# One set of expert lists for four chunks: 39 blocks in three classes in place of 46 in two groups

## The chip, the core and the metric

The kernel runs on one core of a Trainium2 chip. The time is device time of one execution in microseconds (us); the time of a kernel is the median of several executions. A separate execution under the hardware profiler gives the trace. The engines are PE (TensorE, matrix products and transposes, with its weight loads as PEld), DVE (VectorE), ACT (ScalarE), POOL (GpSimd) and SP (SyncE, which here only issues transfers). ACT and POOL issue transfers too: ACT writes results of blocks, POOL does the transfers whose rows are picked by an index. 16 DMA engines carry out all of them.

## What is computed

`x` has 32 x 64 = 2048 tokens of 512 values. Two layers follow each other, each an attention to `ctx_4096` and a feed-forward part. The part that matters here is the last one, a mixture of eight experts, each a 512 x 512 matrix, of which a token uses the best two:

```python
def _L1_ffn_ref(x, W_gate, b_gate, W_e, b_e):
    TOP_K = 2
    logits = x @ W_gate + b_gate
    _, top_idx = jax.lax.top_k(logits, TOP_K)
    y_all = jax.nn.relu(jnp.einsum('bsd,edh->bseh', x, W_e) + b_e)
    y = jnp.take_along_axis(y_all, top_idx[..., None], axis=2)
    return y.mean(axis=2)

x = x + _L0_xattn_ref(_layernorm(x), ctx_4096, ...)
x = x + _L0_ffn_ref(_layernorm(x), ...)
x = x + _L1_xattn_ref(_layernorm(x), ctx_4096, ...)
x = x + _L1_ffn_ref(_layernorm(x), L1_ffn_W_gate, L1_ffn_b_gate, L1_ffn_W_e, L1_ffn_b_e)
```

All data are float32.

## The kernel before

The tokens are handled in four chunks (`NC`) of 512, each of four tiles (`TT`) of 128 tokens. `xs[i]` is tile i of the residual stream, which stays in SBUF. The first attention, the first feed-forward part and the second attention take the kernel up to about 1800 us. The second attention runs as 32 attention blocks, eight for each chunk; the routing of chunk c goes on during the attention blocks of chunk c + 1.

**Routing of a chunk** (`route_step`). Its steps are "rows" (layer norm), "turn" (transpose), "logits", "ranks" (which two experts each token keeps, `keep`) and "places". `route_places` counts, for each expert, how many tokens came before: products with a triangle of ones and with all ones (`cnt`), then running sums (`run`, `counts`, `pos`). `chosen` makes two row numbers for each token from these (`at`): the start of the expert's list in DRAM plus the token's place in it. `route_row` then scatters 128 normed rows into the lists `xg` by these numbers; four tiles and two experts for each token make eight scatters a chunk. They are put on the list `sends` and sent a few at a time.

**Lists and blocks.** The experts' lists are cut into blocks of 128 rows, so that one product of a block uses one expert's matrix. The number of blocks that the loop runs is fixed when the kernel is built, while the counts are only known on the chip; the number is therefore an upper bound, and the last blocks may be empty. There are two groups (`GROUPS`): chunks 0 to 2, and chunk 3, each with its own lists `xg[i]` and results `yg[i]`. `NB` is 2 x 1536 / 128 + 7 = 31 blocks for the first and 2 x 512 / 128 + 7 = 15 for the second. `close_lists(i)` makes a table `bi` on DVE once the counts of a group are complete: for each block its expert and its first row in DRAM. For the first group it stands in the attention block 6 of the last chunk, for the second one in slot 13 of the block loop.

**The block loop.** Slot m loads rows (`load_rows`, every fourth slot for four blocks, on SP, from an address read out of the table), transposes block m (`block_turn`, PE, copied out of PSUM by ACT as `xT`) and multiplies block m - 1 with its expert (`block_expert`): four products on PE into a PSUM bank `py`, of which there are two, the bias added by DVE (`y`), Relu with the factor 0.5 on ACT, and a write to `yg` from ACT's queue. The routing steps of chunk 3 are spread over the first slots (`between`), with one scatter a slot from slot 9 on.

**The way back.** `token_rows` makes, for each token, the two rows of `yg` that hold its results. `gather` fetches them with two indexed transfers of 128 rows from POOL's queue, `combine` adds the two and adds them to the residual on DVE, and SP stores the tile to `out`. The twelve tiles of the first group are gathered one in each slot from slot 34 on and combined two slots later, in three buffers (`t4`); the four tiles of chunk 3 follow after the loop.

**Order.** Work on an engine runs in the order in which the scheduler puts it; what is wrapped in `pin` keeps the order of the program on its engine. Products, transposes, bias adds, sums and all the list arithmetic are pinned. A load by an address from the table waits for all scatters of its group (`add_manual_dep`), and a scatter for the clearing of the lists, which SP does with zeros during the first attention (`clear_lists`).

Of the kernel before, what the change touches and what calls it, by code (L numbers as in the profile page):

```python
# [16 lines left out]
P = 128  # L17
# [12 lines left out]
def layers(ctx: ExitStack, tc: tile.TileContext, a: dict, out: bass.AP):  # L30
# [235 lines left out]
    GROUPS = [range(0, NC - 1), range(NC - 1, NC)]  # L266
    CAP = [len(cs) * CH for cs in GROUPS]
    NB = [2 * cap // P + NE - 1 for cap in CAP]
    xg = [dram.tile([NE * cap, HID], F32, name=f"xg{i}") for i, cap in enumerate(CAP)]
    yg = [dram.tile([nb * P, HID], F32, name=f"yg{i}") for i, nb in enumerate(NB)]  # L270

    start_row = const.tile([P, 2, NE], F32, tag="start_row", name="start_row")
    for i, cap in enumerate(CAP):
        nc.gpsimd.iota(
            start_row[:, i, :], pattern=[[cap, NE]], base=0, channel_multiplier=0,
            allow_small_or_imprecise_dtypes=True,
        )
# [3 lines left out]
    clearings = ([], [])  # L281
    waits = mybir.DependencyInfo(mybir.DependencyClass.Sync, mybir.DependencyReason.DATA)

    def clear_lists(e):
        for i, cap in enumerate(CAP):
            ins = nc.sync.dma_start(
                xg[i][e * cap : (e + 1) * cap, :].rearrange("(p m) (k n) -> p (m k) n", p=P, n=P),
                zero[:, None, :].broadcast_to([P, cap // P * KT, P]),
            )
            clearings[i].append(ins.ins)  # L290
# [338 lines left out]
    for i in range(len(order) + 1):  # L629
# [33 lines left out]
        else:  # L663
# [10 lines left out]
            if i % 4 == 1:  # L674
                clear_lists(i // 4)
# [352 lines left out]
    counts, slots = {}, {}  # L1028
# [33 lines left out]
    def route_places(c, keep):  # L1062

        n = f"e{c}"
        i = 0 if c in GROUPS[0] else 1
# [8 lines left out]
        if i in counts:  # L1074
            pin(nc.vector.tensor_copy(run[:, 0, :], counts[i]))
        else:
            pin(nc.vector.memset(run[:, 0, :], 0.0))
        for t in range(TT):
            pin(nc.vector.tensor_tensor(run[:, t + 1, :], run[:, t, :], tot[:, 1, t, :], ALU.add))
        counts[i] = run[:, TT, :]  # L1080
# [3 lines left out]
        return chosen(pos, keep, start_row[:, i, :], n)  # L1084
# [3 lines left out]
    scatters = ([], [])  # L1088

    def route_row(c, h, at, t, r):  # L1090
        i = 0 if c in GROUPS[0] else 1
        ins = pin(
            nc.gpsimd.indirect_dma_start(
                out=xg[i],
                out_offset=bass.IndirectOffsetOnAxis(ap=at[:, r, t : t + 1], axis=0),
                in_=h[:, t, :],
                in_offset=None,
            )
        )
        for other in scatters[i]:  # L1100
            tc.declare_no_dep(ins.ins, other, reason="rows of a list are distinct")
        for clearing in clearings[i]:
            tc.add_manual_dep(ins.ins, clearing.name, waits, reason="cleared before")
        scatters[i].append(ins.ins)

    def chosen(pos, keep, offset, name):

        q = small.tile([P, TT, NE], F32, tag="q", name=f"q_{name}", bufs=2)
        pin(nc.vector.tensor_tensor(q, pos, offset[:, None, :].broadcast_to([P, TT, NE]), ALU.add))
# [9 lines left out]
    def close_lists(i):  # L1119

        n = f"l{i}"
        top = CAP[i] // P
        lst = small.tile([P, 3, NE], F32, tag="lst", name=f"lst_{n}", bufs=2)
        cmp = small.tile([P, NE, 12], F32, tag="cmp", name=f"cmp_{n}", bufs=1)
        pin(nc.vector.tensor_scalar(lst[:, 2, :], counts[i], 1.0 / P, None, ALU.mult))
        pin(
            nc.vector.tensor_tensor(
                cmp[:, :, 0:top],
                lst[:, 2, :, None].broadcast_to([P, NE, top]),
                steps[:, None, 0:top].broadcast_to([P, NE, top]),  # L1130
                ALU.is_gt,
            )
        )
        pin(nc.vector.tensor_reduce(lst[:, 0, :], cmp[:, :, 0:top], AX.X, ALU.add))
        pin(
            nc.vector.tensor_tensor(
                cmp[:, :, 0:NE], lst[:, 0, None, :].broadcast_to([P, NE, NE]), earlier, ALU.mult
            )
        )
        pin(nc.vector.tensor_reduce(lst[:, 1, :], cmp[:, :, 0:NE], AX.X, ALU.add))  # L1140
        pin(nc.vector.tensor_tensor(lst[:, 2, :], lst[:, 0, :], lst[:, 1, :], ALU.add))

        nb = NB[i]
        own = small.tile([1, 32, NE], F32, tag="own", name=f"own_{n}", bufs=1)[:, 0:nb, :]
        blk = small.tile([1, 4, 32], F32, tag="blk", name=f"blk_{n}", bufs=1)[:, :, 0:nb]
        pin(
            nc.vector.tensor_tensor(
                own,
                lst[0:1, 2, None, :].broadcast_to([1, nb, NE]),
                steps[0:1, 0:nb, None].broadcast_to([1, nb, NE]),  # L1150
                ALU.is_le,
            )
        )
        pin(nc.vector.tensor_reduce(blk[:, 0, :], own, AX.X, ALU.add))
        pin(nc.vector.tensor_scalar(blk[:, 0, :], blk[:, 0, :], float(NE - 1), None, ALU.min))
        pin(
            nc.vector.tensor_tensor(
                own, own, lst[0:1, 0, None, :].broadcast_to([1, nb, NE]), ALU.mult
            )
        )  # L1160
        pin(nc.vector.tensor_reduce(blk[:, 1, :], own, AX.X, ALU.add))
        pin(nc.vector.tensor_tensor(blk[:, 1, :], steps[0:1, 0:nb], blk[:, 1, :], ALU.subtract))
        pin(
            nc.vector.tensor_scalar(
                blk[:, 1, :], blk[:, 1, :], float(top - 1), float(P), ALU.min, ALU.mult
            )
        )
# [12 lines left out]
    def load_rows(i, j0, bi):  # L1180
        xr = t8(f"xr_{i}_{j0}")
        for j in range(j0, min(j0 + 4, NB[i])):
# [6 lines left out]
            for ins in scatters[i]:  # L1189
                tc.add_manual_dep(load.ins, ins.name, waits, reason="all rows are written")  # L1190
# [279 lines left out]
```

## Time and profile before

| | us |
|---|---|
| median of 3 runs | 2008.15 |
| runs | 2007.62 to 2009.62 |
| profiled execution | 2011.58 |
| its span, first to last instruction | 2009.9 |
| PE busy in the span | 1939.5 (96%) |
| 46 products of blocks (`py`), PE busy | 165.8 |
| first transposes of a block | at 1804.29 |
| last bias add of a block | at 1986.85 |
| 32 gathers, first and last issue | at 1933.62 and 2000.40 |

"Busy" is the time in which an engine carries out instructions. Idle time is put down to what ended it, the releaser. The chain of waits follows the work that ended last back through what released it, so that the time on it is time that the end depended on. A window gives the busy time of each engine in a stretch, the clock that TensorE was granted (1.00 is full speed), the mean busy share of the 16 DMA engines and what they moved. That share counts packets, and packets that overlap can take it over 1.

### The profile page before, as it was taken

What the parts mean: (1) busy time and instruction counts of PE and PEld (TensorE: products, weight loads), DVE (VectorE), ACT (ScalarE), POOL (GpSimd) and SP (SyncE); (2) the same over time, 40 slices, a digit from 0 to 9 for tenths busy, and PEclk for the clock granted to TensorE, in tenths of its full rate; (3) what the DMA queues carried; (4) which work ended last, traced back from release to release, by engine and by line L of the source; (5) the groups of instructions that cost most, each with busy time, mean ns of one, the idle gap of its engine ahead of it and who ended that gap; (6) DMA issues with size and microseconds to landing.
All of it is one profiled execution on the core that took longest, in us unless ns stands there. A gap on an engine that the chain in (4) does not pass through costs nothing.

```text
span 2009.9 us, 26460 instructions
## 1 busy us (share of the span) xinstructions
PE 1939.5 (96%) x10576; PEld 1539.5 (77%) x10576; DVE 1014.9 (50%) x1961; ACT 494.4 (25%) x935; POOL 475.0 (24%) x502
## 2 busy tenths in 40 slices
PE   6999999999999999999999999999999999879995
PEld 5888888888888888888888887777787767655442
DVE  7445345345356544444444445364456576762324
ACT  1211111111111221121121122221222655533221
POOL 5111111111122111111111120142145545541024
PEclk8999999999999999999999999999999999989998
DMA  9894110110210110110110013000004101325457
GB/s 320 249 291 131 53 37 16 53 35 19 73 55 21 53 32 22 53 32 22 53 32 22 22 58 105 1 0 11 1 22 157 43 17 53 111 85 183 152 167 231
DMA packets 138234, 155.39 MB, mean 77 GB/s; under 512 B 5121, under 2 KB 88897, under 8 KB 138113
## 3 DMA queue, kind: packets, MB, share of 16 engines
q1 hardware_dynamic: 126096, 124.53, 19.9%
q0 software_dynamic: 5392, 17.11, 2.7%
q10 hardware_dynamic: 6624, 12.06, 1.6%
q8 instruction: 85, 1.39, 0.3%
q14 instruction: 37, 0.30, 0.1%
HBM read 94.44 MB, written 58.20 MB: 76 GB/s over the span
## 4 chain that ended last, share of the span: by engine, by line
PE 90%; DVE 6%; ACT 2%; POOL 1%; issue 1%; DMA 1%; POOLq 0%; SPq 0%; DVEq 0%; ACTq 0%
PE ppx_o L425 11%; PE pqx_a L425 8%; PE py L105 8%; PE sc_a L105 6%; PE pqz_a L425 6%; PE pv_a L105 6%; PE ppz_o L425 5%; PE pk_a L105 5%; PE po_o L105 3%; PE ppy_o L425 3%; PE pdx_f L425 3%; PE pqv_a L425 3%; PE pqy_a L425 3%; PE pp L105 3%; PE phx_f L425 2%; PE pq_b L105 1%
## 5 line engine op out<-in xcount | busy, mean ns | idle before, releaser
L105 PE MATMUL py<-arena,xT 128*128 x368 | 165.8, 593 | 0.2 <-ACT xT L1200 0.2
L407 POOL TENSOR_TENSOR arena<-weights 128x512 f32<-128x512 f32 x16 | 20.3, 1269 | 563.2 <-PE ppz_o L425 563.2
L366 ACT ACTIVATE at_a<-at_a 128x512 f32<-128x512 f32 x64 | 40.4, 631 | 444.0 <-DVE at_a L365 444.0
L105 PEld LDWEIGHTS pv_a<-weights,arena 128*128 128x128 f32 x1024 | 119.4, 192 | 15.3 <-issue 15.3
L425 PE MATMUL pqz_a<-arena 128*128 128x256 f32 x512 | 122.8, 383 | 4.4 <-DVE qT_a L501 4.4
L105 PEld LDWEIGHTS sc_a<-kT_a,qT_a 128*128 128x128 f32 x1024 | 122.7, 196 | 1.8
L425 PE MATMUL ppx_o<-weights,oT_o 128*128 128x256 f32 x512 | 122.8, 383 | 0.1
L105 PE MATMUL sc_a<-kT_a,qT_a 128*128 128x64 f32 x1024 | 121.0, 278 | 0.0
L425 PE MATMUL pqx_a<-arena,weights 128*128 128x256 f32 x512 | 121.0, 379 | 0.0
L494 ACT ACTIVATE u_a<-pqx_a,bq 128x256 f32<-128x256 f32 x192 | 80.6, 471 | 163.1 <-PE pqx_a L425 163.1
L105 PE MATMUL pv_a<-weights,arena 128*128 128x128 f32 x1024 | 119.5, 275 | 0.0
L105 PEld LDWEIGHTS py<-arena,xT 128*128 128x128 f32 x368 | 66.2, 190 | 66.0 <-issue 65.5
L105 PE MATMUL pk_a<-arena,weights 128*128 128x512 f32 x256 | 115.2, 593 | 0.0
L425 PEld LDWEIGHTS pqz_a<-arena 128*128 128x128 f32 x512 | 98.3, 192 | 18.3 <-issue 4.7
L479 DVE COPY v_a<-pv_a 128x512 f32<-128x512 f32 x32 | 22.1, 692 | 178.6 <-PE pv_a L105 178.6
L585 DVE TENSOR_TENSOR x<-ppx_o,x 128x512 f32<-128x512 f32 x128 | 86.9, 679 | 45.6 <-PE ppx_o L425 43.8
L425 PEld LDWEIGHTS ppx_o<-weights,oT_o 128*128 128x128 f32 x512 | 94.8, 190 | 12.0 <-ACT oT_o L575 0.5
L425 PEld LDWEIGHTS pqx_a<-arena,weights 128*128 128x128 f32 x512 | 94.8, 190 | 11.6
L501 DVE TENSOR_TENSOR qT_a<-pqz_a,u_a 128x512 f32<-128x512 f32 x64 | 44.2, 691 | 112.2 <-ACT u_a L494 80.2
L1218 DVE TENSOR_TENSOR y<-py,weights 128x512 f32<-128x512 f32 x46 | 31.8, 692 | 120.6 <-PE py L105 113.8
L105 PEld LDWEIGHTS pk_a<-arena,weights 128*128 128x128 f32 x256 | 48.5, 191 | 47.4 <-issue 45.9
L397 POOL TENSOR_TENSOR arena<-weights 128x512 f32<-128x512 f32 x18 | 22.8, 1267 | 249.4 <-PE pqz_a L425 246.0
(337 smaller groups left out, 3826.3 us busy)
## 6 DMA issues: line engine op xcount, KB each, us to landing
xg<-zero SPq DMA_DIRECT2D x8, 3072.0 KB
weights<-in_Wq SPq DMA_DIRECT2D x16, 1024.0 KB
weights<-in_Wo SPq DMA_DIRECT2D x16, 1024.0 KB
xr<-xg SPq DMA_DIRECT2D x46, 256.0 KB
yg<-y ACTq DMA_DIRECT2D x46, 256.0 KB
weights<-in_Wkv SPq DMA_DIRECT2D x32, 256.0 KB
arena<-in_ctxT SPq DMA_DIRECT2D x8, 1024.0 KB
xg<-zero SPq DMA_DIRECT2D x8, 1024.0 KB
```

Of the source, the lines that this page charges most:

```text
L105: nc.tensor.matmul(ps, lhsT, rhs, start=(i == 0), stop=(i == len(pairs) - 1))
L366: nc.scalar.activation(dst, dst, AF.Exp, scale=scale)
L397: engine.tensor_tensor(s1, a21, a22, ALU.add)
L407: engine.tensor_tensor(t1, b12, b11, ALU.subtract)
L425: nc.tensor.matmul(ps[:, m, :], left[:, k, m * P : (m + 1) * P], right[:, k, :], start=first and m == i == k == 0, stop=i == len(pairs) - ...
L479: nc.vector.tensor_copy(v, pv)
L494: nc.scalar.activation(u[:, m * 256 : (m + 1) * 256], ps[:, m * 256 : (m + 1) * 256], AF.Identity, bias=bq[:, 4 * g + 2 * heads + m : 4 * ...
L501: nc.vector.tensor_tensor(q5[:, heads, :, 4 * half : 4 * half + 4, :], ps.rearrange("p (m b q) -> p m b q", m=2, q=64), u.rearrange("p (m ...
L585: nc.vector.tensor_tensor(dst, ps.rearrange("p (m n) -> p m n", m=2), dst, ALU.add)
L1218: pin(nc.vector.tensor_tensor(y, py, be1[:, bass.ds(v[1], 1), :], ALU.add))
```

## The change

The two groups become one set of lists. `xg` holds, for each expert, room for all 2048 tokens, and `counts` runs through all four chunks. The blocks fall into three classes, which follow each other in the order of the slots:

- full: blocks that chunks 0 to 2 fill up whole. At least `FULL` = 17 exist, so that slots 0 to 16 are always of this class;
- begun: blocks that chunks 0 to 2 begin and don't fill up, at most eight. Full and begun together are at most `COVER` = 31;
- the last chunk's: what chunk 3 adds beyond these. All together are at most `NB` = (4096 + 8 x 127) / 128 = 39 blocks.

`close_full` makes the table for slots 0 to 16 where `close_lists(0)` stood, `close_rest` makes the table for slots 17 to 38 in slot 9. Loads of slots 0 to 16 don't wait for chunk 3's scatters, since these write other rows; loads from slot 17 on wait for all 32 scatters. Chunk 3's "places" step moves from slot 9 to slot 8, and two scatters go out a slot in place of one. `token_rows` runs for one chunk in each of the slots 17 to 20. A token's row depends on whether its place lies in a block of its chunk's earlier class or a later one, which adds five operations a chunk.

The gathers of chunks 0 to 2 start in slot 31 and read rows of slots 0 to 30 alone; two tiles in even slots, one in odd ones. Their sums follow two slots behind. The buffers are five pieces of `weights`, which is no longer used, in place of three `t4` tiles and two `t8` tiles. After the loop, each of chunk 3's four tiles is gathered, with one waiting sum after each.

The core of the diff:

```diff
-    GROUPS = [range(0, NC - 1), range(NC - 1, NC)]
-    CAP = [len(cs) * CH for cs in GROUPS]
-    NB = [2 * cap // P + NE - 1 for cap in CAP]
-    xg = [dram.tile([NE * cap, HID], F32, name=f"xg{i}") for i, cap in enumerate(CAP)]
-    yg = [dram.tile([nb * P, HID], F32, name=f"yg{i}") for i, nb in enumerate(NB)]
+    FIRST = (NC - 1) * CH
+    FULL = -(-(2 * FIRST - NE * (P - 1)) // P)
+    COVER = (2 * FIRST + NE * (P - 1)) // P
+    NB = (2 * T + NE * (P - 1)) // P
+    xg = dram.tile([NE * T, HID], F32, name="xg")
+    yg = dram.tile([NB * P, HID], F32, name="yg")
...
-    scatters = ([], [])
+    scatters, full_loads = {c: [] for c in range(NC)}, []
...
+        if c == NC - 1:
+            for load in full_loads:
+                tc.declare_no_dep(ins, load, reason="rows of full blocks are others")
...
-    def close_lists(i):
...
+    def whole_blocks(dst, count, op, name):
+
+        cmp = t2(f"cmp_{name}")[:, 0 : NE * 16].rearrange("p (e t) -> p e t", e=NE)
+        first = 1 if op == ALU.is_ge else 0
+        scaled = small.tile([P, NE], F32, tag="scaled", name=f"sc_{name}", bufs=2)
+        pin(nc.vector.tensor_scalar(scaled, count, 1.0 / P, None, ALU.mult))
+        pin(
+            nc.vector.tensor_tensor(
+                cmp, scaled[:, :, None].broadcast_to([P, NE, 16]),
+                steps[:, None, first : first + 16].broadcast_to([P, NE, 16]), op,
+            )
+        )
+        pin(nc.vector.tensor_reduce(dst, cmp, AX.X, ALU.add))
...
+    def lay_class(k, before, name):
+
+        tmp = t2(f"lay_{name}")[:, 0 : NE * NE].rearrange("p (e f) -> p e f", e=NE)
...
+        pin(nc.vector.tensor_reduce(slot[:, k, :], tmp, AX.X, ALU.add))
+        if before is not None:
+            pin(nc.vector.tensor_scalar(slot[:, k, :], slot[:, k, :], before, None, ALU.add))
+        pin(nc.vector.tensor_tensor(shift[:, k, :], slot[:, k, :], block[:, k, :], ALU.subtract))
+        pin(nc.vector.tensor_scalar(shift[:, k, :], shift[:, k, :], float(P), None, ALU.mult))
+
+    def class_slots(j0, j1, classes, name):
...
+        nb, ns = j1 - j0, classes * NE - 1
...
+        for i in range(2):
+            pin(
+                nc.vector.tensor_tensor(
+                    own,
+                    ends[:, 0, None, :].broadcast_to([1, nb, ns]),
+                    steps[0:1, j0:j1, None].broadcast_to([1, nb, ns]),
+                    ALU.is_le,
+                )
+            )
+            pin(
+                nc.vector.tensor_tensor(
+                    own, own, ends[:, 1 + i, None, :].broadcast_to([1, nb, ns]), ALU.mult
+                )
+            )
+            pin(nc.vector.tensor_reduce(at[:, i, :], own, AX.X, ALU.add))
...
+    def close_full():
+
+        pin(nc.vector.memset(block[:, 0, :], 0.0))
+        whole_blocks(num[:, 0, :], counts[NC - 2], ALU.is_ge, "full")
+        whole_blocks(block[:, 2, :], counts[NC - 2], ALU.is_gt, "cover")
+        pin(nc.vector.tensor_copy(block[:, 1, :], num[:, 0, :]))
+        pin(nc.vector.tensor_tensor(num[:, 1, :], block[:, 2, :], num[:, 0, :], ALU.subtract))
+        lay_class(0, None, "0")
+        return class_slots(0, FULL, 1, "full")
+
+    def close_rest():
+
+        whole_blocks(num[:, 2, :], counts[NC - 1], ALU.is_gt, "all")
+        pin(nc.vector.tensor_tensor(num[:, 2, :], num[:, 2, :], block[:, 2, :], ALU.subtract))
+        total = small.tile([P, 2], F32, tag="total", name="total", bufs=1)
+        pin(nc.vector.tensor_reduce(total[:, 0:1], num[:, 0, :], AX.X, ALU.add))
+        pin(nc.vector.tensor_reduce(total[:, 1:2], block[:, 2, :], AX.X, ALU.add))
+        lay_class(1, total[:, 0:1], "1")
+        lay_class(2, total[:, 1:2], "2")
+        return class_slots(FULL, NB, 3, "rest")
...
-            load = nc.sync.dma_start(xr[:, j - j0, :], xg[i][bass.ds(v, P), :])
-            for ins in scatters[i]:
-                tc.add_manual_dep(load.ins, ins.name, waits, reason="all rows are written")
+            load = nc.sync.dma_start(xr[:, j - j0, :], xg[bass.ds(v, P), :]).ins
+            for c in range(NC):
+                for ins in scatters[c]:
+                    if j < FULL and c == NC - 1:
+                        tc.declare_no_dep(load, ins, reason="rows of full blocks are others")
+                    else:
+                        tc.add_manual_dep(load, ins.name, waits, reason="all rows are written")
...
+    def send_back(c, t):
+        nonlocal back
+        ys = weights[:, 1, back % 5 * 1024 : (back % 5 + 1) * 1024]
+        back += 1
+        ys = ys.rearrange("p (r n) -> p r n", r=2)
+        gather(c, t, slots[c], ys)
+        waiting.append((c, t, ys))
...
-        if sends:
-            route_row(*sends.pop(0))
-        if m == 13:
-            lists.append([*close_lists(1)])
-        elif m == 15:
-            rows_of = [token_rows(i, lists[i][1]) for i in range(2)]
-        if m > first + 2 and done < len(GROUPS[0]) * TT:
...
-        while waiting and (len(waiting) > 2 or m == len(blocks)):
-            combine(*waiting.pop(0))
+        for _ in range(2):
+            if sends:
+                route_row(*sends.pop(0))
+        if m == 9:
+            tables[FULL] = close_rest()
+        elif m > 16 and m - 17 < NC:
+            slots[m - 17] = token_rows(m - 17)
+        if m >= COVER and left:
+            for _ in range(2 - m % 2):
+                if left:
+                    send_back(*left.pop(0))
+        for _ in range(2 - m % 2 if COVER + 2 <= m < NB else 0):
+            combine(*waiting.pop(0))
...
     for t in range(TT):
-        gather(1, 0, t, rows_of[1], ys[t // 2][:, 2 * (t % 2) : 2 * (t % 2) + 2, :])
-    for t in range(TT):
-        combine(NC - 1, t, ys[t // 2][:, 2 * (t % 2) : 2 * (t % 2) + 2, :])
+        send_back(NC - 1, t)
+        combine(*waiting.pop(0))
+    while waiting:
+        combine(*waiting.pop(0))
```

## The prediction

> **What bounds the kernel now.** I read the page first, then the chain of waits, then the timeline and the windows from 1780 us on, because both programs were built with the same order on every engine up to there, apart from the clearing of the lists.
>
> ```profile
> span 2009.9 us, 26460 instructions
> PE 1939.5 (96%) x10576; PEld 1539.5 (77%) x10576; DVE 1014.9 (50%) x1961; ACT 494.4 (25%) x935; POOL 475.0 (24%) x502
> ```
>
> The reader is to see one engine at 96%: work that leaves PE is worth its full length unless something else takes the place. The chain's last pieces (start, us, what):
>
> ```profile
> 1976.08 3.44 PE py L105 x8
> 1979.95 6.88 PE py L105 x16
> 1986.85 0.70 DVE y L1218
> 1987.58 0.64 ACT y L1219
> 1988.24 2.07 DMA yg<-y
> 1990.42 0.70 issue
> 1991.12 0.95 POOL ys L1224
> ...
> 2000.40 4.92 DMA ys<-yg,at_l
> 2005.42 0.70 DVE ys L1233
> 2006.15 0.69 DVE x L1234
> ```
>
> Two stages: blocks on PE back to back until 1986.85, then a tail of 4.27 us to the first gather of the last chunk and 18.8 us from there to the end (2009.9 - 1991.12). Block 33 has its products at 1937.35 and block 44 at 1979.95 in the chain: 42.6 / 11 = 3.873 us a block, of which 3.44 are the eight py matmul passes and 0.44 the transposes.
>
> The stage ahead of the blocks, in the timeline (start, us, engine, line, operation, idle before and releaser):
>
> ```profile
> 1786.40 0.67 DVE L951 TENSOR_REDUCE mx_b<-sc_b 128x8 f32<-128x512 f32 x1
> 1788.44 0.57 ACT L991 COPY mix<-po 128x512 f32<-128x512 f32 x1
> 1789.06 1.99 PE L105 MATMUL pp<-weights,mix_last 128*128 128x256 f32 x8 [1.80 <-ACT mix L991]
> ```
>
> Here PE is not the bound: the softmax of the last attention block (mx_b) waits in DVE's order behind close_lists, and PE waits for ACT.
>
> **The blocks removed.** 46 - 39 = 7 blocks x 3.873 = 27.1 us off PE, on the path. The built order of the changed program has 39 groups of py matmuls, in the same order between the attention and block 7; then cnt_e stands one block earlier, at no change in length. That all 39 follow at 3.873 needs their inputs in time, see the waits below.
>
> **close_full in place of close_lists(0).** It stands at the same place, ahead of mx_b. 27 DVE operations in place of 16, so 11 more. Dependent small ones start 0.2 us apart (blk_l at 1785.58, 1785.79, 1785.89, 1786.08, bi_l at 1786.29); the six table operations shrink from 1x248 (0.39 to 0.60) to 1x119 (0.27 by the 1x120 rows of the second list), six x 0.27 = 1.6 for four that took 1.79; the 128x128 compares take about 0.30 (128x96 took 0.26). So 11 x 0.2 - 0.2 = **+2.0 us**. From below 11 x 0.10 = 1.1, the spacing of independent ones (1780.83, 1780.89, 1781.02); from above 11 x 0.42 = 4.6, the pace beside POOL's mix operations (six from 1782.64 to 1785.15). Second, ACT's built order now has both Exp of that attention block ahead of the copy of mix (L991) for which pp waits. The second Exp's input is ready at 1788.50 + 0.69 = 1789.19, and 0.63 later the copy starts at 1789.85 instead of 1788.44: **+1.4** (from below 0). PE runs through from pp to the blocks only behind that copy, with no slack between, so both go to the path: +3.4, bounds 1.1 to 6.0. Late next: pt_v, the last mix, the last pp, block 0, everything by as much.
>
> **close_rest and token_rows, inside the blocks.** close_rest is 32 operations: six on 1x506 at about 0.69 (0.27 at 120, 0.40 at 248 elements) and 26 x 0.2, together 9.3 us in four slots, beside the bias add of 0.69. By the built order the adds of blocks 9 and 10 come up to 1.3 and 2.4 us late. Behind the add wait ACT's Relu, the yg write and the py bank; PE asks for that bank again 4.3 us after it ends (one block and the transposes), so 4.3 - 0.8 = 3.5 us late is free. Zero; without that bank each us over 3.5 would count. From above, another 2 us late beside POOL (as for close_full) is 0.9 over. token_rows: 4 x 11 x 0.2 in four slots of 3.87, zero by the same cover.
>
> **The scatters and the load of block 17.** The places are laid one slot earlier and go out two a slot, and SP's load of block 17 now waits for all eight and for the second table. Scatters issue 1.28 us apart (1846.87 to 1855.84 before); with +3.4 and one slot less, the last lands near 1858, and the table is cast near 1860. Behind the wait on SP stand only further loads; blocks 12 to 16 are ahead of it. Block 17's transposes are due at 1871.1 + 3.4 = 1874.5, the load takes some 2.4 us (a yg write of that size took 2.07 plus 0.33 issue): 12 us of slack. Zero; each us beyond 12 would count whole. The clearing keeps its bytes (8 x 4 MB for 8 x 3 and 8 x 1 MB).
>
> **The gathers.**
>
> ```profile
> 1933.62 0.99 POOL L1224 DMA_INDIRECT ys<-yg,at_l  x1 [76.81 <-PE px L1197]
> 1934.92 0.98 POOL L1224 DMA_INDIRECT ys<-yg,at_l  x1 [0.30 <-issue]
> ```
>
> The first gather goes out when block 30 is written, and block 30 is the last one that the first three chunks need after the change too: 1933.62 + 3.4 = 1937.0. One gather costs POOL 1.26 us (0.96 and 0.30). 24 of them used to lie in 12 blocks at two a block; now 24 x 1.26 = 30.2 end at 1967.2, while block 38 is written at 1991.12 - 27.1 + 3.4 = 1967.4. So POOL just keeps up, with 0.2 us to spare. Five tile slots hold them back less than three did: the sixth tile's gathers wait for the first sum. Each sum is a new wait on DVE, nearer behind its gathers (about 2.5 us after the second one's issue in the tail, 1993.34 to 1995.86); behind it stands the next bias add, with the 3.5 us of cover. 1.5 sums x 1.37 + 0.69 = 2.7 of 3.87 us busy.
>
> What is short is the DMA engines. Windows (busy by engine, clock, DMA share, GB/s) and queues from 1950 to 1986:
>
> ```profile
> 1958.00:1966.00 8.00, 8.00 (x26) 3.85 (x25) 4.22 (x7) 2.23 (x4) 3.82 (x4) 1.00 0.82 267
> 2002.00:2006.00 4.00, 0.00 (x0) 0.00 (x0) 1.96 (x3) 0.00 (x0) 0.00 (x0) 0.50 0.58 213
> 2006.00:2010.00 4.00, 0.00 (x0) 0.00 (x0) 0.81 (x2) 0.00 (x0) 0.00 (x0) 0.50 0.30 112
> ```
> ```profile
> q0 software_dynamic: 1419, 4.67, 44.3%
> q1 hardware_dynamic: 1296, 2.36, 18.0%
> q10 hardware_dynamic: 1297, 2.36, 17.2%
> ```
>
> With 18 gathers, 9 stores of out and 9 writes of yg in 36 us these are 0.886, 0.72 and 0.69 us of all 16 engines each. Per block: 2 x 0.886 + 0.72 + 0.69 = 3.18 of 3.87, the 0.82 seen. After: 3 x 0.886 + 1.5 x 0.72 + 0.69 = 4.43 of 3.87, or 1.14: more than there is. From 1937 on there remain 32 gathers, 16 stores, 8 writes: 28.4 + 11.5 + 5.5 = 45.4 us, of which the last 8 us take 3.5 (0.58 and 0.30 x 4). 41.9 us in the 40.2 us from 1938 to 1986.2 - 8 is a share of 1.04. The start of the same trace held 0.98 (2 to 10 us) to 1.10 (30 to 40 us) with large loads. At 0.97 it is 43.2 us, **+3.0**. From below 41.9 / 1.10 = 38.1, nothing; from above 41.9 / 0.83, the busiest window of this phase, 50.5 us: +10.3. I take 0.97 because a queue that never runs dry is nearer to the start than to a phase that asked for 0.82.
>
> The trace moves 361, 377 and 364 GB/s in the three windows from 10 to 40 us. [...] The sum goes by the rows' shares.
>
> **Sum.** 2009.9 - 27.1 + 3.4 + 3.0 = 1989.2 us of span, 20.7 less. The profiled execution took 2011.58 with 1.7 around the span, the runs 2007.62 to 2009.62 with a median of 2008.15: 2008.15 - 20.7 = **1987.5 us**, with the bounds of the two costs 2008.15 - 27.1 + 1.1 = 1982.2 to 2008.15 - 27.1 + 6.0 + 10.3 = 1997.4.
>
> **Rivals.** (1) The transfers are hidden anyway: packets overlap to a share of 1.10 and POOL's pace decides. For it, the start of the trace; against it, rows gathered by index. 2008.15 - 27.1 + 3.4 = 1984.5, or 1981.1 if the attention's end has slack that I don't see. 17%. (2) Gathers keep the pace of the tail: pairs were summed at 1995.86, 1998.58, 2003.5 and 2005.42, 9.56 / 6 = 1.6 us each with stores beside. 32 x (1.6 - 1.26) = 10.9 for the 3.0: 1995.4. Against it, the tail waits for latency as well. 11%. (3) The load of block 17 comes late and uses up its 12 us and ten more: 1997.5. Against it, every wait there has a row. 5%. (4) Slower: the gathers take the slowest pair's pace, 1998.58 to 2003.5, 2.46 us each, in the whole phase; each sum then holds DVE, the adds and PE's banks behind it. 32 x 1.20 = 38.4: 2008.15 - 27.1 + 3.4 + 38.4 = 2022.9. It decides from 23.7 / 32 = 0.74 over 1.26, 2.0 us a gather; against it, 1.6 is the mean. 6%. That the blocks are not really fewer is out: the built order shows 39.
>
> **How the numbers follow.** The forecast has 61%. It and rivals 1 to 3 are faster, 94% less a little for a near miss; rival 4 is slower. A measurement of this kernel tells some 0.2%, 4 us, from no change, and only an unlikely middle (pace near 2.0) falls inside. The range 1980.5 to 1995 holds the forecast but for its far upper end, and rival 1.
>
> **What would show it.** After: 39 blocks at 3.87 us; block 0 some 3.4 us later, with DVE's mx_b near 1788.4; a DMA share of 0.95 or more between 1940 and 1968; sums that wait for gathers; a last-chunk first gather near 1967 to 1970. Wrong if the first px of block 17 waits for SP, if PE idles between blocks by more than 3 us in all, or if gathers stand over 2 us apart.

## The result, and the profile after

The changed kernel takes 1999.13 us (median of 7 runs, 1997.02 to 2003.78) beside 2008.28 for the kernel before, measured with it: a ratio of 0.9952, 95% interval 0.994 to 0.9965. It is faster, as forecast, but by 9.2 us in place of 20.7, and 1999.13 lies above the range of 1980.5 to 1995. The profiled execution, one of the seven, took 1999.48. From its page, and the third line's counterpart from the page of before:

```profile
span 1997.6 us, 26205 instructions
PE 1913.1 (96%) x10492; PEld 1523.6 (76%) x10492; DVE 1019.1 (51%) x1999; ACT 487.2 (24%) x921; POOL 475.8 (24%) x501
L105 PE MATMUL py<-arena,xT 128*128 x312 | 142.3, 599 | 5.7 <-issue 4.5
yg<-y ACTq DMA_DIRECT2D x39, 256.0 KB
```
```profile
L105 PE MATMUL py<-arena,xT 128*128 x368 | 165.8, 593 | 0.2 <-ACT xT L1200 0.2
```

The third line is the group of the blocks' products: busy time, mean of one in ns, and the idle time ahead of them. 312 products are 39 blocks; 368 were 46. But PE idled 5.7 us ahead of them (0.2 before), 4.5 of it in one piece, and one product took 599 ns in place of 593. The last line of the first fence counts transfers; a third number, the time to landing, is missing there, and that becomes a clue.

The chain of waits (start, us, what) shows where:

```profile
1947.61 0.44 PE px L1270 x4
1948.05 3.44 PE py L105 x8
1951.48 0.44 PE px L1270 x4
1951.92 4.49 issue
1956.40 5.25 PE py L105 x8
...
1970.91 6.47 DMA weights<-yg,at_r
...
1987.76 4.96 DMA weights<-yg,at_r
```

Up to 1951.92 the blocks follow at 3.87 us. Then PE stands still for 4.49, with nothing in the records that it would wait for, and the next eight products take 5.25 in place of 3.44.

The spans, cut at the same events. The last column is explained with the experiments: the same kernel, run again.

| from, to (us of difference to the kernel before) | forecast | after | same kernel, h1 |
|---|---|---|---|
| start to the first `pp` of the last pair (1785.27 before) | 0 | -1.8 | -2.1 |
| from there to block 0's transposes (19.02 before) | +3.4 | +4.8 | +4.8 |
| 7 blocks x 3.873 | -27.1 | -27.1 | -27.1 |
| block 0's transposes to the last product, beyond that | part of +3.0 | +7.5 | +0.5 |
| last product to the first gather of the last chunk (4.30 before) | part of +3.0 | +4.4 | +6.0 |
| from there to the end (18.78 before) | 0 | -0.1 | 0.0 |
| span | -20.7 | -12.3 | -17.9 |

The miss of 8.4 us in the span is 11.9 - 3.0 of the gathers' term and 4.8 - 3.4 of close_full's, less the 1.9 of rows 1 and 6. In the medians some 3 us more are missing: I took it that the changed kernel's profiled run would stand as far above its median as that of before did, 3.4 us; it stands 0.3 above. 1.8 of that are row 1, attention that the change does not touch and that was slow in that one execution of the kernel before.

**The stage ahead of the blocks**, in the timeline after (start, us, engine, line, operation, idle before and releaser):

```profile
1786.72 0.67 DVE L952 TENSOR_REDUCE mx_b<-sc_b 128x8 f32<-128x512 f32 x1
...
1790.08 0.57 ACT L992 COPY mix<-po 128x512 f32<-128x512 f32 x1
...
1790.70 3.78 PE L105 MATMUL pp<-weights,mix_last 128*128 128x256 f32 x8 [5.26 <-ACT mix L992]
```

close_full lasts 7.6 us (1779.12 to 1786.72) where close_lists took 5.6: +2.0. ACT's copy starts 3.36 after mx_b where it started 2.04 after: +1.3. Both are the sizes forecast. With them PE's idle time grows from 1.80 to 5.26. What comes on top is in the last line too: the products behind it took 3.78 in place of 1.99. The windows (length, busy by PE, PEld, DVE, ACT, POOL, then clock, DMA share, GB/s), after and then before:

```profile
1790.00:1795.00 5.00, 4.30 (x12) 3.48 (x13) 0.48 (x2) 1.48 (x4) 3.13 (x5) 0.50 0.00 2
```
```profile
1789.00:1794.00 5.00, 4.41 (x32) 2.91 (x32) 3.13 (x7) 2.57 (x7) 3.33 (x5) 1.00 0.01 2
```

The granted clock is 0.50 in place of 1.00. The window from 1788.00 to 1790.70 has a clock of 0.66, with 1.00 up to 1788.50 and 0.50 from 1789.00 on, which puts the fall some 3.4 us after PE's last product ended at 1785.44. In e7 the eight products behind 2.90 us of idle time took 5.40 in place of 3.60. In the kernel before, 1.80 us left it at 1.00 (1789 to 1794).

**The stall.** ACT's copies xT, which PE's products need, in the timeline after, with POOL's gathers and DVE's bias add:

```profile
1944.21 0.59 ACT L1272 COPY xT<-px 128x512 f32<-128x512 f32 x1 [2.76 <-PE py L105]
...
1955.76 0.58 ACT L1272 COPY xT<-px 128x512 f32<-128x512 f32 x1 [9.93 <-remote]
...
1958.86 0.95 POOL L1299 DMA_INDIRECT weights<-yg,at_r  x1 [0.30 <-issue]
...
1962.21 0.69 DVE L1291 TENSOR_TENSOR y<-py,weights 128x512 f32<-128x512 f32 x1 [8.25 <-PE px L1270]
1962.21 0.59 ACT L1272 COPY xT<-px 128x512 f32<-128x512 f32 x1 [5.33 <-PE px L1270]
...
1963.77 1.28 POOL L1299 DMA_INDIRECT weights<-yg,at_r  x1 [3.96 <-DVE weights L1308]
```

The copy waits for nothing but the signal that PE has finished its transposes. Those of block 36 ended at 1948.04 by the chain, and the copy starts at 1955.76, 7.7 us later; ACT had nothing else to do. Those of block 37 ended at 1951.92, and copy and bias add, on two engines, start together at 1962.21. All that time POOL issued gathers without a pause: 18 of them, most 1.26 us apart, from 1936.69 to 1959.81. Five tile buffers let it run ahead of the slots that the program gives them. It stops when it needs a buffer that a sum has to free; the sum stands in DVE's order behind the bias add, which waits for PE's signal. 2.4 us after POOL's last gather ends, the signals of block 37 arrive; that of block 36 had come at 1955.76, while POOL was still issuing.

The kernel before had a smaller case, which I passed over. Eight scatters ran in a row there from 1846.87 to 1856.81:

```profile
1852.19 0.59 ACT L1200 COPY xT<-px 128x512 f32<-128x512 f32 x1 [2.76 <-issue]
...
1855.84 0.97 POOL L1093 DMA_INDIRECT xg<-h_e,at_e  x1 [0.31 <-issue]
...
1857.49 0.59 ACT L1200 COPY xT<-px 128x512 f32<-128x512 f32 x1 [4.18 <-PE px L1197]
```

ACT's idle time ahead of a copy is 2.76 in a steady block; behind the eighth scatter it is 4.18.

### The profile page after: what moved, and what is told of

It is laid out like the page before. It is cut to its first block, busy times and chain, and to the rows that moved or that the text cites. A ratio compares the mean times of both kernels' runs of the same rounds, so it can differ in the third digit from the quotient of the medians.

```text
span 1997.6 us, 26205 instructions
## 1 busy us (share of the span) xinstructions
PE 1913.1 (96%) x10492; PEld 1523.6 (76%) x10492; DVE 1019.1 (51%) x1999; ACT 487.2 (24%) x921; POOL 475.8 (24%) x501
## 4 chain that ended last, share of the span: by engine, by line
PE 89%; DVE 6%; ACT 2%; issue 1%; DMA 1%; POOL 1%; POOLq 0%; SPq 0%; DVEq 0%; ACTq 0%
PE ppx_o L426 11%; PE pqx_a L426 8%; PE py L105 6%; PE sc_a L105 6%; PE pv_a L105 6%; PE ppz_o L426 6%; PE pqz_a L426 5%; PE pk_a L105 5%; PE po_o L105 3%; PE pdx_f L426 3%; PE ppy_o L426 3%; PE pp L105 3%; PE pqv_a L426 3%; PE pqy_a L426 3%; PE phx_f L426 2%; PE pq_b L105 1%
## 5 line engine op out<-in xcount | busy, mean ns | idle before, releaser
L105 PE MATMUL py<-arena,xT 128*128 x312 | 142.3, 599 | 5.7 <-issue 4.5
L105 PEld LDWEIGHTS py<-arena,xT 128*128 128x128 f32 x312 | 56.7, 192 | 62.8 <-issue 61.1
L502 DVE TENSOR_TENSOR qT_a<-pqy_a,u_a 128x512 f32<-128x512 f32 x32 | 22.1, 691 | 114.9 <-PE pqy_a L426 114.9
```

The source lines that it names most:

```text
L105: nc.tensor.matmul(ps, lhsT, rhs, start=(i == 0), stop=(i == len(pairs) - 1))
L502: nc.vector.tensor_tensor(q5[:, heads, :, 4 * half : 4 * half + 4, :], ps.rearrange("p (m b q) -> p m b q", m=2, q=64), u.rearrange("p (m ...
```

## The experiments

Three theories were at stake. **A, traffic:** the DMA engines are asked for more than they can do, as the prediction had it. **P, POOL:** a long unbroken run of indexed transfers on POOL holds up PE's signals. **C, close_full:** its place ahead of a softmax costs what the stage ahead of the blocks grew by, and more. Each time is a median of 4 to 10 executions and each ratio is to the kernel before, run beside it; the fourth column has the idle time of PE between the products of blocks, and the last one numbers the chips.

| kernel | us | ratio (95%) | PE idle in one piece | chip |
|---|---|---|---|---|
| e1_one_tile | 1996.48 | 0.9943 (0.9926 to 0.9959) | 4.01 | 1 |
| e2_half_rows | 1996.24 | 0.9935 (0.9918 to 0.9952) | 6.03 | 1 |
| e3_stores_late | 2000.31 | 0.9957 (0.994 to 0.9973) | 8.90 | 1 |
| e4_close_late | 1995.94 | 0.9937 (0.992 to 0.9953) | 8.13 | 1 |
| e5_three_bufs | 2004.5 | 0.9973 (0.9962 to 0.9984) | 4.07, 4.12 | 2 |
| e6_gated | 1998.21 | 0.9944 (0.9927 to 0.9961) | 1.64, 5.09 | 2 |
| e7_close_b7 | 1992.23 | 0.9907 (0.9891 to 0.9924) | 2.90, 4.57 | 2 |
| e8_before_six | 2011.4 | 1.0006 (0.9997 to 1.0016) | 1.60 | 2 |
| f1_paced_close | 1986.27 | 0.989 (0.9873 to 0.9906) | none | 3 |
| f2_paced | 1990.41 | 0.9919 (0.9903 to 0.9936) | none | 3 |
| f3_few_rows | 1997.23 | 0.9945 (0.9928 to 0.9961) | 4.49 | 3 |
| g1_plain | 1985.38 | 0.9867 (0.9843 to 0.9892) | none | 4 |
| h1_after_again | 1994.44 | 0.9933 (0.9916 to 0.9949) | 0.22 | 5 |
| h2_plain_again | 1984.34 | 0.9878 (0.9861 to 0.9894) | none | 5 |
| h3_paced_close_again | 1986.29 | 0.9884 (0.9867 to 0.99) | none | 5 |
| k1_after | 1999.74 | 0.9955 (0.9941 to 0.9968) | 4.53 | 6 |
| k2_paced | 1991.41 | 0.9907 (0.9892 to 0.9922) | none | 6 |
| k3_close_b7 | 1992.77 | 0.9916 (0.9903 to 0.993) | 1.00, 5.82 | 6 |

**Less traffic: e2 and e3.** e2 fetches half of each row, e3 keeps the stores of `out` back until the loop is over:

```diff
-                out=ys[:, r, :],
+                out=ys[:, r, 0:256],
...
-                in_=yg[0 : slots_of * P, :],
+                in_=yg[0 : slots_of * P, :].rearrange("r (h n) -> (r h) n", h=2),
```
```diff
-        nc.sync.dma_start(out[(c * TT + t) * P : (c * TT + t + 1) * P, :], x)
+        if c == NC - 1 or done:
+            store(c, t)
+        else:
+            held.append((c, t))
...
+    for at in held:
+        store(*at)
```

> Each gather fetches 1 KB of a row in place of 2 KB (the first half of yg, read as rows of 256), the other half of the sums is left out of what is fetched; the number of gathers and of their rows and the pace of 1.26 us are kept. Theory A1 (bytes): 1.02 MB per slot in place of 1.41, no gap, last py near 1963, last chunk's first gather near 1968, time 1986 to 1989. Theory A2 (the number of gathered rows, not their bytes): the gap of 4 to 5 us stays, time 1996 to 1999.

> The twelve stores of chunks 0 to 2 stand behind the loop on SP's queue; gathers, sums and their pace are as in the changed kernel. Theory A1 (bytes of all kinds): 1.02 MB per slot, no gap, last py near 1963, yg of block 38 lands in 3 to 4 us, then 3 MB of stores lie beside the last gathers (at some 340 GB/s 9 us): 1986 to 1992. Theory A3 (the gathers' own traffic, stores do not matter): gap and late py stay, and the stores come on top at the end: 1999 to 2004.

Neither takes the stall away. In e2 it is longer, 6.03 us, in a window with a DMA share of 0.56 (after has 0.91 there):

```profile
1950.00:1960.00 10.00, 3.97 (x12) 1.89 (x11) 2.02 (x3) 1.11 (x2) 7.56 (x9) 0.87 0.56 167
```

Theory A falls as the cause of the stall. The times of e2 and e3 lie within 3 us of the changed kernel's, one on each side.

**Gathers one tile a slot, fewer buffers, or gated: e1, e5, e6.** e1 gathers and sums one tile in every slot and leaves the rest to the end of the loop; e5 has three tile buffers; e6 lets a gather of chunks 0 to 2 wait for the bias add two blocks ahead of its slot:

```diff
-            for _ in range(2 - m % 2):
-                if left:
-                    send_back(*left.pop(0))
+            send_back(*left.pop(0))
```
```diff
-        ys = weights[:, 1, back % 5 * 1024 : (back % 5 + 1) * 1024]
+        ys = weights[:, 1, back % 3 * 1024 : (back % 3 + 1) * 1024]
```
```diff
+            if c < NC - 1:
+                tc.add_manual_dep(ins.ins, biases[-2].name, waits, reason="its slot")
```

> One tile a slot is fetched and one summed, in place of three in two slots; what is left of chunks 0 to 2 is fetched behind the loop. DMA demand in the slots falls from 1.41 MB per 3.87 us (256 KB of yg, 768 KB of gathers, 384 KB of stores) to 1.02 MB. Theory A (the changed kernel's 4.5 us of idle TensorE and its slow landings come from more traffic than the 16 queues move): TensorE runs the 39 blocks without a gap, the last py ends near 1963 in place of 1970; four or five tiles are left behind the loop, 8 to 10 gathers of 1.26 us, so that the last chunk's first gather is near 1975 and the time 1994 to 1998. Theory B (the stall has nothing to do with the gathers' pace, it comes from the code of blocks 35 to 37 or from the clock): the gap at block 36 stays, the last py ends near 1970, and the time is 2000 to 2006.

> Three buffers for the gathered tiles in place of five: GpSimd stops after 6 gathers until a sum frees a buffer. Theory P (while GpSimd issues gathers of 1.26 us without a break, TensorE's signals reach ScalarE and VectorE late; in the five profiles so far the first free signal came 1.9 to 2.8 us after GpSimd had run out of buffers): GpSimd pauses after some 8 us, no xT copy waits over 4 us, TensorE idles under 1 us between blocks, the last py ends near 1963 to 1964, the last chunk's gathers begin near 1968 to 1972, time 1989 to 1994. Theory Q (any gather beside the blocks, or these blocks' code, makes the gap): the gap of 4 to 9 us before py of block 36 stays, 1997 to 2002.

> Five buffers, but each slot's gathers wait for the bias add of the block before last, so that three gathers go out in 3.87 us on average and never more than the slots' own. Theory P with the break as what counts: three gathers of 1.26 us fill 3.78 of 3.87 us, GpSimd has next to no break, but a late signal stops the gathers within a slot or two: lateness of 2 to 4 us in place of 10, time 1992 to 1997. Theory P with the run ahead of the slots as what counts: no gap, 1988 to 1992. Theory Q: the gap of 4 to 9 us stays, 1997 to 2002.

In e1 the stall stays (4.01): the place in the program's order paces nothing, POOL still ran 16 gathers in a row, as far as the buffers reached. e5 was not the experiment that I meant: with three buffers the gather of a tile stands ahead of the sum of the tile three before it, so its sums add rows of a later tile and wait for them; it tells nothing between the theories. e6 alone leaves two stalls, 1.64 and 5.09: three tiles in two slots are 3.8 us of gathers a slot of 3.87, so the gate held POOL nowhere in its first 18 gathers, which followed each other without a pause (1933.62 to 1957.07).

**Paced by dependency: f2 and k2** join e1 and e6: one tile a slot, and no gather ahead of its slot.

> The same pace without moving close_full. Theory P: no gap, last py near 1963 to 1964, the last chunk's first gather near 1970, time 1989 to 1991. Theory Q: 1997 to 2000. The difference to the run with both edits is the price of close_full's place: theory C 5 to 7 us, theory D under 2.

> One tile a slot held back by the bias add, close_full where the change has it. With late signals on this chip: 7 to 10 us under the changed kernel. Without: y of block 38 no longer waits behind a sum (3.8 us) and its landing is as before; the gathers left behind the loop cost some of it: 2 to 5 us under the changed kernel, 1989 to 1992 in both cases.

No stall is left; k2 is 8.3 us under the unchanged k1 on the same chip (1991.41 and 1999.74). The products of blocks on the pages of k1 and k2:

```profile
L105 PE MATMUL py<-arena,xT 128*128 x312 | 143.7, 603 | 4.8 <-issue 4.5
```
```profile
L105 PE MATMUL py<-arena,xT 128*128 x312 | 140.6, 593 | 0.2 <-ACT xT L1272 0.2
```

The timeline of f1, which is paced in the same way, shows signals late by up to 2.7 us. A late bias add then holds POOL's next gather, and beside the blocks the runs are of 10 and 6 gathers (12 and 4 in f2, 10 and 6 in k2) in place of 18:

```profile
1945.73 0.58 ACT L1272 COPY xT<-px 128x512 f32<-128x512 f32 x1 [5.12 <-remote]
1946.01 1.16 POOL L1303 DMA_INDIRECT weights<-yg,at_r  x1 [2.00 <-DVE y L1292]
```

**The run of gathers in the kernel before: e8.** The kernel before, with six tile buffers in place of three:

```diff
-            ys = t4(f"ys_{u}_{t}")
+            at = done % 6 * 1024
+            ys = weights[:, 1, at : at + 1024] if at < 5120 else weights[:, 0, 4096:5120]
```

> The kernel before with six buffers for the gathered tiles in place of three, all else as it was: GpSimd issues 12 gathers of 1.26 us without a break at first, then two a slot. Theory P: TensorE's signals come late from the eighth or tenth gather on, near 1944, a gap of 2 to 6 us between two blocks, time 2009 to 2014. Theory Q (the code of the changed kernel's last blocks): no gap, 2007 to 2009.

```profile
1942.74 0.69 DVE L1218 TENSOR_TENSOR y<-py,weights 128x512 f32<-128x512 f32 x1 [5.55 <-remote]
...
1945.55 0.59 ACT L1200 COPY xT<-px 128x512 f32<-128x512 f32 x1 [7.55 <-PE px L1197]
...
1946.18 3.70 PE L105 MATMUL py<-arena,xT 128*128 x8 [1.60 <-issue]
```

On this chip a longer run of gathers made the signals late, with none of the change's lists or slots. The run was of 12 gathers (1929.24 to 1944.13). The time can't be told from before (1.0006, 0.9997 to 1.0016): the stall of 1.6 us would be 1.0008.

**Fewer rows in flight: f3.** Half the rows of a gather, 64, at nearly the same cost on POOL (1.22 us each):

```diff
-                out=ys[:, r, :],
+                out=ys[0:64, r, :],
...
-                in_offset=bass.IndirectOffsetOnAxis(ap=at[:, r, t : t + 1], axis=0),
+                in_offset=bass.IndirectOffsetOnAxis(ap=at[0:64, r, t : t + 1], axis=0),
```

> The changed kernel with gathers of 64 rows in place of 128 (the other 64 tokens of each tile get what the buffers held), as many gathers and no break between them. If the rows in flight are what counts (the stall began after some eight gathers, 1024 rows): it begins after some sixteen gathers, so at most one late signal, gap under 2 us, time 1988 to 1993. If the unbroken run of gathers on GpSimd counts, whatever their rows: late signals from the eighth gather on, gap 4 to 9 us, 1996 to 2000, unless the gather itself becomes much shorter than 1.26 us, which the profile tells.

```profile
1958.24 4.63 PE L105 MATMUL py<-arena,xT 128*128 x5 [4.49 <-issue]
```

The same 4.49 us of idle as after, with 18 gathers in a row: neither the bytes (e2) nor the rows (f3) that the gathers move decide.

**Plain transfers in place of gathers: g1, and h2 with h1 beside it.** The same bytes on POOL's queue, without an index, so that the sums add rows of other tokens. One costs POOL 0.54 us, and the longest run in g1 is nine of them, 4.9 us:

```diff
+            k = (c * TT + t) * 2 + r if c < NC - 1 else NB - 1 - 2 * t - r
+            ins = nc.gpsimd.dma_start(ys[:, r, :], yg[k * P : (k + 1) * P, :])
```

> The changed kernel with each gather replaced by a plain copy of one block of yg into the same buffer, issued by GpSimd in the same places and no earlier than block 30 is written (the sums then add rows of other tokens): the same 256 KB, the same buffers, no row indices. Theory P1 (the signals are held back by the gathers' row-wise transfers that GpSimd prepares): no xT copy waits over 4 us, no gap, last py near 1963, last chunk's first copy near 1968, 1985 to 1990. Theory P2 (any unbroken run of DMAs issued by GpSimd does it): late signals from the eighth copy on, gap of 4 us or more, 1994 to 2000.

> The changed kernel once more, beside the plain copies. Theory P1 (the kind of transfer): gap of 4 us or more before py of block 36, late signal at the scatters, 1997 to 2001. Theory R (the chip of the plain copies' run did it): were this chip like that one, no gap and 1987 to 1990.

> Plain copies of blocks in place of the gathers once more (the sums add rows of other tokens). Theory P1: no late signal in the last slots, 1984 to 1988. Theory R: a gap as in the changed kernel, 1994 to 2000.

h2 shows no stall, at a higher DMA share than the phase had with gathers:

```profile
1950.00:1960.00 10.00, 10.00 (x31) 4.88 (x30) 6.56 (x11) 3.05 (x6) 4.29 (x8) 1.00 1.04 411
```

PE is busy for the whole window at a share of 1.04, which is theory A's second failure. But h1, the unchanged kernel on that chip, has no stall either, with the same unbroken gathers. So this pair doesn't say whether the index matters, and it shows that the stall is not in the kernel alone: an unbroken run, 24 gathers here, is not enough. The page of h1:

```profile
span 1992.0 us, 26205 instructions
L105 PE MATMUL py<-arena,xT 128*128 x312 | 140.8, 593 | 0.5 <-ACT xT L1272 0.2
yg<-y ACTq DMA_DIRECT2D x39, 256.0 KB, 2.7
```

There the time to landing (2.7 us) is present that is missing after. The traces that have late signals lack records of transfers' completions (after: 4136 of 4736 are there, 16 for each of 296 transfers; before: 4675 of 5088); of those without late signals, h1, g1 and h2 have all 4736 and h3 has 4729. In after none of the 2080 up to 1640 us is missing; POOL's first indexed transfer goes out at 1658.7, and the missing ones all lie behind. The third run of the unchanged kernel, on another chip than h1's, has the stall again:

> The changed kernel, third time. If its profile shows late signals (TensorE's signals reaching ScalarE 4 us or more late after the eighth gather): 1997 to 2001. If not: 1993 to 1996.

```profile
1953.87 6.66 PE L105 MATMUL py<-arena,xT 128*128 x8 [4.53 <-issue]
```

The unchanged kernel thus stands at 0.9952 and 0.9955 where signals are late, and at 0.9933 (0.9916 to 0.9949) where they aren't. The medians differ by 4.7 to 5.3 us, though the intervals overlap a little. Why one chip or execution has it and another not stays open. Each execution on record has the span and the clock that the profiler gives, so no run tells whether signals come late where nothing is recorded.

**What remains without late signals**, in the timeline of h1:

```profile
1959.18 3.67 PE L105 MATMUL py<-arena,xT 128*128 x8 [0.22 <-DVE y L1291]
...
1964.85 0.69 DVE L1308 TENSOR_TENSOR weights<-weights 128x512 f32<-128x512 f32 x1 [1.04 <-DMA weights<-yg,at_r]
...
1966.60 0.69 DVE L1291 TENSOR_TENSOR y<-py,weights 128x512 f32<-128x512 f32 x1 [0.33 <-issue]
...
1967.98 0.33 ACTq L1293 DMA_DIRECT2D yg<-y  x1
...
1973.19 0.95 POOL L1299 DMA_INDIRECT weights<-yg,at_r  x1 [4.29 <-DMA yg<-y]
```

Block 38's products end at 1962.85, and its bias add comes at 1966.60, 3.75 us later: DVE's order has two sums ahead of it, and the second waits for its gathers. The write to `yg` takes 4.4 us from its issue to landing at 1972.38, and the first gather that needs it goes out at 1973.19. Within the blocks sums held PE for 0.22 us only. After waits for the same write:

```profile
1971.03 0.68 DVE L1291 TENSOR_TENSOR y<-py,weights 128x512 f32<-128x512 f32 x1
...
1972.40 0.33 ACTq L1293 DMA_DIRECT2D yg<-y  x1
...
1978.89 0.95 POOL L1299 DMA_INDIRECT weights<-yg,at_r  x1 [6.96 <-DVE x L1309]
```

Its add comes 0.9 us after the last product, and the last packet of ACT's queue ends at 1977.74, 5.3 us after the write's issue; the gather follows 1.15 later. In h1 and in before 1.21 us lie between that packet and that gather. The trace names DVE's sum as the releaser and the chain above follows it, but the record of this landing is not there, and h1's gather starts ahead of the same sum (1973.19 and 1973.62). By the last packet the write takes 1.7 us where POOL's last gather ended over 4 us before it (before, e5, e7, e8, k3) and 3.0 to 5.7 in all other traces (h1 4.0), so behind the blocks the transfers in flight do seem to cost time; no run separates gathers from stores there.

**close_full elsewhere: e4, e7 and k3.** e4 puts it behind the whole attention, e7 and k3 one attention block later than the change:

```diff
-        if c == NC - 1 and b == 6:
+        if i == NI:
             tables[0] = close_full()
```
```diff
-        if c == NC - 1 and b == 6:
+        if c == NC - 1 and b == 7:
             tables[0] = close_full()
```

> close_full stands behind the last attention block in place of before its scores. Theory C (close_full ahead of mx_b of block 7 costs the path ahead of block 0, some 5 us: 5.3 us of idle TensorE at the mix copy, then matmuls at a lower clock): block 0's px comes 4 to 6 us earlier, mx_b directly behind at_b, the time falls by as much, 1993 to 1996. Theory D (the blocks' start is set by something else, such as the route or the loads of block 0): px moves by less than 1.5 us, 1998 to 2000. Should the loads of block 0 become late, 2 to 4 us are given back.

> close_full one attention block later, behind the scores' maxima of block 7 (mx_b) in VectorE's order. Theory C: the 5.3 us of idle TensorE at the mix copy go, and the low clock behind them; block 0's loads are there in time (in the run with close_full at the end the px of block 0 waited 3.3 us for them); px of block 0 some 20 us after the first pp of the last pair in place of 23.8, time 1995 to 1996 with the stall at block 36 as it was. Theory D: px as in the changed kernel, 1998 to 2000.

> close_full behind mx_b of block 7, the gathers as in the change: 4 to 7 us under the changed kernel of this chip, whether signals come late or not.

```profile
1782.90 3.72 PE L105 MATMUL pp<-weights,mix_last 128*128 128x256 f32 x16 [0.52 <-POOL mix_last L1000]
...
1799.90 1.04 PE L1270 MATMUL px<-ident,xr 128*128 128x128 f32 x8
```

In e7 PE's idle time ahead of `pp` is 0.52 in place of 5.26, and from there to block 0 it takes 17.0 us in place of 23.8 (16.5 in k3; 19.0 before). k3 is 7.0 us under k1. The last `pp` took 6.42 in e7 and 6.43 before, so the 2.0 us between these two are not its clock: the list work's place had cost time in the kernel before as well. In e4 block 0 starts late for its loads, 3.32 us of idle ahead of its first transposes, and its stall is 8.13, so its time says little. Theory C holds.

**Both together: f1 and h3** are f2 with e7's edit.

> One tile (two gathers) a slot, held back until the bias add of the block before last, three tiles behind the loop, and close_full behind mx_b of block 7. Theory P (gathers without a break hold TensorE's signals back, two a slot with a break of 1.3 us do not, as in the kernel before): no gap, the last py ends near 1956 (block 0's first py near 1801 and 38 x 3.873 + 7), the 24th gather near 1962, the last chunk's first near 1963, 18.7 us more to the end: span 1981 to 1984, time 1983 to 1986. Theory Q: a gap of 4 us or more stays at block 36 or 37, time 1989 to 1993.

> One tile a slot held back by the bias add, and close_full behind mx_b of block 7, once more: 1984 to 1988, 10 to 14 us under the changed kernel of the same chip.

They take 1986.27 and 1986.29 us, ratios 0.989 (0.9873 to 0.9906) and 0.9884 (0.9867 to 0.99), on a chip with late signals and on one without: 12.9 us under the changed kernel's 1999.13. On h3's chip, where nothing stalls, it is 8.2 us under h1, not the 10 to 14 expected. On the chip of f1 and f2, close_full's place is worth 4.1 us (1990.41 to 1986.27), under the 5 to 7 expected, and their intervals touch; k3 and k1 show it more clearly. That is the version to keep.

## Why the prediction was right and wrong

- **Blocks removed, -27.1:** right. 39 groups of products, 3.873 us apart wherever nothing stalls.
- **close_full, +3.4:** the mechanism and both parts were right (+2.0 and +1.3 measured), the term was mis-sized: +4.8. Missing was that with PE's idle time of 5.26 us the clock would fall to 0.50, so that eight products cost 1.8 us more. The last `pp` took 5.41 in place of 6.43, which is not the change's doing: e8, with the list work as before, has 5.41, and e3, with it as in the change, 6.78. 4.8 is within the bounds given.
- **close_rest, token_rows, scatters, the load of block 17, all at nothing:** no wait of PE shows in h1 in these slots.
- **Gathers, +3.0 (0 to 10.3): the step that failed.** The first gather at 1936.69 (1937.0 forecast) and its 1.26 us on POOL were right. The rest was costed by DMA share, and beside the blocks shares were not what decided: a share of 1.04 ran without a stall (h2), a share of 0.56 with one (e2). The 11.9 us measured, over the upper bound of 10.3, consist of 7.5 within the blocks, from PE's signals that came late during an unbroken run of gathers, and 4.4 behind them, 0.9 from block 38's add and the rest from its write, 5.3 us in place of 1.7. In h1, without late signals, the same two parts are 0.5 and 6.0. Why signals come late on some chips stays open. I had written that PE idling over 3 us between blocks would show the prediction wrong; it idled 4.49 in one piece.
- **"The bias add behind a sum has 3.5 us of cover":** right within the blocks (0.22 us of idle in h1), wrong for block 38. The cover was PE's next use of the bank, and the last block has no next use: its add feeds the path. That, and a write that lands in 4.4 us (2.07 before), make 6.0 of h1's 6.5.
- **The rate of the transfers:** 404 GB/s in g1 and 411 in h2 (1950 to 1960), above the 361 to 377 in the trace of before (10 to 40 us).
- **Rivals:** none of them named the mechanism. Rival 4's (sums that hold adds behind them) is seen for the last add alone, at 3.7 us and not 38.4. Rival 3's time (1997.5) is nearest, but its wait did not come; rival 2's (1995.4) is next, but most gathers in the run kept 1.26 us a piece, not 1.6. Rival 1's hidden transfers hold for h1's blocks and not for its end.
- **Sum:** the two unknown costs at their upper ends together gave 1997.4, 1.7 under the result. The range stopped short of its own bounds.

## What to carry to other kernels

Here the buffer count paced the queue, not the place in the program (16 gathers in a row in e1, with one tile a slot). So give transfers that may run ahead a dependency on their slot, with fewer of them in a slot than the queue can issue in it (e6 lacked that: 3.8 us of gathers a slot of 3.87), and keep runs on one queue short (PE did not idle behind runs of up to 12 gathers in f1, f2 and k2, and idled 4.49 us in one piece behind 18 in after). Look at the idle time ahead of an operation that recurs each block, such as 2.76 that becomes 4.18: it showed a late signal in the kernel before, where PE idled only 0.2 us ahead of its blocks' products. Cover by a later use ends with the last iteration (block 38's add came 3.75 us behind its products in h1), and list work belongs behind the last softmax that PE waits for, not ahead of it (PE's idle time ahead of `pp` was 0.52 in e7 and 5.26 in after).

## What the runs showed of the hardware that was not expected

Signals from PE reached ACT 7.7 and 10.3 us late while POOL issued 18 indexed transfers in a row (after), and up to 12.2 us late in e7 (due at 1949.09, copy at 1961.32). The second of two came 2.0 to 2.8 us after POOL stopped (2.4 after, 2.0 in e1, 2.8 in e2 and e4, 2.5 in e3 and k1); the first often came while POOL was still issuing (at 1955.76 in after, with POOL's last gather at 1958.86). The first signal over 1 us late was due 11.3 us after a run of gathers began, with nine of them issued (after, e1 to e4), and 9.2 us after a run of scatters began (before). With the same program chip 5 showed none of it (24 gathers in a row in h1, 0.22 us of PE idle time), and on chip 4 (g1) eight scatters in a row delayed nothing (the copies xT stayed 3.87 us apart from 1852.15 to 1859.89). TensorE's clock stood at 0.50 after 5.26 us without work, so that the idle time's growth of 3.5 us cost 1.8 us on top.
